# A depthwise convolution in six of eight blocks: from twelve TensorE passes to one projection, scaled copies on ScalarE and sums on GpSimd

## The chip, the cores and the metric

The kernel runs on one core of a Trainium2 chip. A core has TensorE (matrix multiply, PE in the profile, its weight loads PEld), VectorE (DVE), ScalarE (ACT), GpSimd (POOL) and SyncE (SP), which here issues every DMA. The metric is the device time of one execution in microseconds; several runs are taken, and the median counts. The profile is of one such execution.

## What is computed

Two layers over x of 4 sequences x 1024 positions x 128 channels in float32, each of the form x + s * silu(f), with s and f taken from the layer-normalised x. In the first layer s is a retention (a causal attention with decay) and f a gated network of five ternary matrices. In the second, f routes the better half of the positions through a network with a Gelu, and s is a state-space block. The part that matters here is the start of that block:

```python
x_and_gate = x @ W_in + b_in
x_ssm, gate = jnp.split(x_and_gate, 2, axis=-1)
xc = jnp.transpose(x_ssm, (0, 2, 1))
xc = lax.conv_general_dilated(xc, conv_w[:, None, :], window_strides=(1,),
        padding=[(K_ - 1, 0)], feature_group_count=D, ...) + conv_b[None, :, None]
x_conv = silu(jnp.transpose(xc, (0, 2, 1)))
BC = x_conv @ W_x + b_x
B_mat, C_mat = jnp.split(BC, 2, axis=-1)
...
h = A_discrete[None] * h + xc_t[:, :, None] * B_t[:, None, :]
y = jnp.einsum('bn,bdn->bd', C_t, h) + D_param * xc_t
...
y = y * silu(gate)
y = y @ W_out + b_out
```

So: a projection, a convolution of each channel with 4 taps back in time (zeros before the sequence), a Silu, the projections B and C, and a scan over time with 16 states for each of 128 channels.

## The kernel before

The 4096 positions are cut into 8 blocks of 512, two to a sequence (j is the block, g = 0 or 1 its place in the sequence). In most of the kernel channels or states lie on the 128 partitions and the 512 positions along the free axis. Each block goes through the same stages: ln0, retention, gated, hidden1, hidden2, out0 (the first layer), ln1, front, states, gates, router, moe, scans, project, finish, and for each sequence ranks.

The stages only record operations. A planner (Plan, lines 174 to 376) then puts them in order: it keeps for each engine the operations that can start, and picks by estimated time, then by priority. The priority comes from TIMES (lines 60 to 78), a length and eight starts for each stage; an operation inherits the lowest priority of what needs it. It also hands out buffers, a fixed number for each tag. The instructions of each engine are issued in that order and stay in it, so an instruction that waits holds up all behind it on its engine. Since all of them are issued in one loop at line 373, the profile gives them all that line, and they are told apart by the names of their tiles.

What the change touches:

- ln1 (line 793) leaves the normalised block transposed as two rounded parts, xh and xl, each with 3 columns of the block before ahead of its 512. A float32 product is made of three passes of a rounded format: high weights with high part, high weights with low part, low weights with high part (three_pass, line 676).
- front (line 812) makes the convolution in px, a PSUM bank: for each of 4 taps the input projection with that tap's weights folded in (wcv, 4 x 128 columns), on the block moved by the tap, three passes each, 12 passes of 128 x 512. At the start of a sequence the bias that the zeros would have brought in is taken off 3 columns on VectorE (edges). ScalarE's Silu, with the folded bias cbias, writes xc, and a DMA stores it to xd in DRAM.
- states (line 828) makes B and C from xc. In blocks 0 and 7 (BY_PE) TensorE spreads them over the partitions. In blocks 1 to 6, pb on TensorE is written as bc by ScalarE, stored to bd, read back spread into Br and Cr by two DMAs, and Br is copied into the one PSUM bank B by ScalarE. The tag Br has one buffer.
- scans (line 921) does 16 scans of 128 x 512 for each block. Its u tiles (two scans each, 6 buffers) are loaded from xd by DMA, multiplied by B on VectorE (u<-u,B), scanned on VectorE, multiplied by Cr on GpSimd (u<-u,Cr), and summed over the states on TensorE into py. ScalarE copies the last column (last) for the next block of the sequence. In block 7 (U_BY_PE), the first four u come from TensorE instead (pu), with the constant rep.
- gated and hidden1 split each Gelu or Silu result into parts: ScalarE casts the high part (h_h, g_h), GpSimd subtracts for the low part (h_l, g_l), and the pa and pb passes on TensorE read both.

Of the kernel before, what the change touches and what calls it, by code (L numbers as in the profile page):

```python
# [45 lines left out]
_CST = {}  # L46
_n = 0
for _name, _w in (
    ("ident", P), ("mask", P), ("tie", P), ("sel", P), ("rowdec", 1), ("coldec", 1),
):  # L50
    _CST[_name] = (_n, _n + _w)
    _n += _w
NCST = _n


ORDER = mybir.DependencyInfo(mybir.DependencyClass.NoSync, mybir.DependencyReason.DATA)
# [1 line left out]


TIMES = {  # L60
    "ln0": (10.465, (-34.463, 37.568, 0.307, -8.702, 29.140, 25.837, -0.706, 2.276)),
    "retention": (7.697, (19.747, 29.540, 0.054, 5.261, 0.588, -0.481, 27.669, 17.510)),
    "gated": (0.198, (17.080, -12.778, -2.899, 37.127, 52.075, 3.684, 35.848, 24.681)),
    "hidden1": (181979.521, (10.669, -0.997, 0.654, 26.140, 49.753, 13.692, 29.323, 21.440)),
    "hidden2": (104.604, (6.706, 7.824, 35.607, 17.363, 7.255, 8.335, 12.787, 23.305)),
    "out0": (0.269, (-10.144, 10.621, 13.685, 32.888, 37.354, 6.208, 14.587, 34.725)),
    "ln1": (0.086, (-3.447, -9.822, 3.389, 39.108, 24.646, 10.527, 7.924, 19.641)),
    "front": (99775.310, (31.104, -7.375, 49.241, 35.721, 3.625, 15.911, 8.435, 28.268)),
    "states": (1929558528.870, (-22.925, -12.719, -2.927, -2.692, -1.385, 5.843, 8.364, 33.960)),
    "gates": (2802.502, (-10.124, -3.354, -1.683, 3.017, 7.752, 67.130, 11.212, 9.313)),  # L70
    "router": (35.459, (32.003, 36.047, 1.039, 23.096, 29.397, 12.314, 55.205, 9.245)),
    "moe": (0.850, (-6.037, 10.367, -2.942, 3.023, 8.714, 12.982, 45.904, 32.432)),
    "ranks": (3.658, (7.924, -5.386, 32.363, 0.750, 18.387, 5.771, 15.184, 9.739)),
    "scans": (0.083, (26.879, 6.452, 3.058, 25.041, 26.277, 9.568, 13.774, 14.948)),
    "project": (0.218, (-2.585, 1.221, 6.521, 8.046, 9.527, 12.283, 10.650, 21.658)),
    "finish": (2311.973, (10.042, -1.800, 14.285, 18.479, 29.156, 18.433, 18.474, 24.699)),
    "load_x": (0.107, (32.705, -1.570, 6.609, 55.729, 2.835, 7.712, 33.265, 51.716)),
}
SWITCH = 0.725
SPARE = 2  # L80
XB = 5
BY_PE = (0, NBK - 1)
U_BY_PE = (NBK - 1,)
# [298 lines left out]
def tile_kernel(  # L382
# [34 lines left out]
    for name, n in {  # L417
        "x": XB, "stat0": 2, "ve0": 2, "rs0": 2, "tm0": 2, "stat1": 2, "ve1": 2, "rs1": 2, "tm1": 2, "col": 2, "wm": 2, "most": 2, "eq": 2,
        "nxt": 2, "xn0": 2, "xnT": 1, "qT": 1, "vd": 1, "sT": 1, "st": 1, "y": 1,
        "sc": 1, "xh0": 2, "xl0": 2, "sO": 2, "xh1": 2, "xl1": 2, "Br": 1, "Cr": 2, "bc": 1,  # L420
        "gate": 2, "xc": 2, "cmp": 2, "a": 3, "xn1": 3, "ff": 3, "so": 3,
        "hh": 8, "hl": 8, "h2": 5, "u": 6, "last": 2,
    }.items():
        early = name in ("a", "h2")
        plan.tag(sb, name, n, early or name in ("hh", "hl", "u"), 1 if early else None)

    def tile_(tag, name, shape=(P, HB), dtype=F32):
        if tag == "const":
            tag = name
            plan.tag(sb, tag, 1)  # L430
        return plan.tile(tag, shape, dtype, name)
# [42 lines left out]
    def vcopy(o, i):  # L474
        n = o.length() if psum(i, o) else o.length() / 2
        do("vector", "tensor_copy", o, i, cost=(n + 66) / 960)
# [20 lines left out]
    def load(name, src, shape, tag="const"):  # L497
        t = tile_(tag, name, shape)
        dma(t, src)
        return t  # L500
# [8 lines left out]
    place(-3.0)  # L509
    load_x(0)  # L510
    vec = load("vec", vecs, (P, NVEC))
    cs = load("cs", cst, (P, NCST))
    wqk_s = load("wqk_s", wqkT, (P, 2 * D), "sT")

    by_state = lambda a: a.rearrange("(e n) k -> n e k", n=NS)
    A_log = load("A_log", by_state(vecs[:, slice(*_VEC["A_log"])]), (P, NSC))
    w12_s = load("w12_s", w12T, (P, 2 * F), "sc")
    wv_t = load("wv_t", wv, (P, D))
    sel = load("sel", by_state(cst[:, slice(*_CST["sel"])]), (P, P))
    h_s = [  # L520
        [load(f"{nm}_s{k}", src[k * P : (k + 1) * P, :], (P, F), "h2") for k in range(KC)]
# [26 lines left out]
    def c(name):  # L548
        a, b = _CST[name]
        return cs[:, a:b]  # L550
# [51 lines left out]
    wB, wC = (tile_("const", name, (P, P)) for name in ("wB", "wC"))  # L602
    for w, i in ((wB, 0), (wC, NS)):
        vcopy(w.split(NS), wx_t[:, i : i + NS].stretch(E))

    rep_t = tile_("const", "rep", (P, 4 * P))
    rep = [rep_t[:, i * P : (i + 1) * P] for i in range(4)]
    for i in range(4):
        vcopy(rep[i].split(NS), c("ident")[:, 4 * i * E : (4 * i + 1) * E].repeat(NS))
    vcopy(A, logA)  # L610
    vcopy(tie, c("tie"))
    wg = split(win_s[:, D : 2 * D], "wg", (P, D))

    wcv_s = tile_("ff", "wcv_s", (P, 4, D))
    a, b = _ROW["conv_w"]
# [60 lines left out]
    def three_pass(w, xhl, cols=slice(None)):  # L676

        (wh, wl), (xh, xl) = w, xhl
        return [(wh[:, cols], xh), (wh[:, cols], xl), (wl[:, cols], xh)]
# [132 lines left out]
    def front(j):  # L812

        b, g = divmod(j, NH)
        px = mm_tile(f"px_{j}")
        terms = []
        for k in range(4):
            hi, lo = (t[:, k : k + HB] for t in R[j]["parts"])
            terms += three_pass(wcv, (hi, lo), slice(k * D, (k + 1) * D))
        passes(px, terms)  # L820
        if not g:
            vtt(px[:, 0:3], px[:, 0:3], edges, ALU.subtract)
        xc, xd = tile_("xc", f"xc_{j}"), tile_("xd", f"xd_{j}")
        act(AF.Silu, xc, px, bias=cbias)
        dma(xd, xc)
        R[j].update(xc=xc, xd=xd)

    def states(j):
        xc = R[j]["xc"]
        if j in BY_PE:  # L830
            Bp, Cr = tile_("B", f"B_{j}"), tile_("Cr", f"Cr_{j}")
            mm(Bp, wB, xc, True, True)
            if j in U_BY_PE:
                R[j]["Br"] = Br = tile_("Br", f"Br_{j}")
                act(AF.Identity, Br, Bp, bias=bB)
            act(AF.Identity, Bp, Bp, bias=bB)
            pC = mm_tile(f"pC_{j}")
            mm(pC, wC, xc, True, True)
            act(AF.Identity, Cr, pC, bias=bC)
        else:  # L840
            pb = mm_tile(f"pb_{j}", (2 * NS, HB))
            mm(pb, wx_t, xc, True, True)
            bc, bd = tile_("bc", f"bc_{j}", (2 * NS, HB)), tile_("bd", f"bd_{j}", (2 * NS, HB))
            act(AF.Identity, bc, pb, bias=v("b_x", 0, 2 * NS))
            dma(bd, bc)
            Br, Cr = tile_("Br", f"Br_{j}"), tile_("Cr", f"Cr_{j}")
            dma(Br, bd[0:NS, :].each(E), 0.63, 2.24e5)
            dma(Cr, bd[NS : 2 * NS, :].each(E), 0.63, 2.24e5)
            Bp = tile_("B", f"B_{j}")
            copy(Bp, Br)  # L850
        R[j].update(B=Bp, Cr=Cr)
# [69 lines left out]
    def scans(j):  # L921

        b, g = divmod(j, NH)
        xc, xd, Bp, Cr = (R[j][k] for k in ("xc", "xd", "B", "Cr"))
        py = tile_("py", f"py_{j}")
        last = prev.get("last")
        if not g:
            prev["last"] = tile_("last", f"last_{j}", (P, NSC))
        for m in range(4):
            us = []  # L930
            for q in range(0, 4, 2):
                ks = [4 * q + m, 4 * (q + 1) + m]
                u = tile_("u", f"u_{j}_{ks[0]}", (P, 2, HB))
                if m == 0 and j in U_BY_PE:
                    for i, k in enumerate(ks):
                        pu = mm_tile(f"pu_{j}_{k}")
                        mm(pu, rep[q + i], xc, True, True)
                        vtt(u[:, i, :], pu, R[j]["Br"], ALU.mult)
                else:
                    for i, k in enumerate(ks):  # L940
                        dma(u[:, i, :], xd[k * E : (k + 1) * E, :].whole(NS), 0.63, 2.24e5)
                    vtt(u, u, Bp.repeat(2), ALU.mult)
                for i, k in enumerate(ks):
                    do("vector", "tensor_tensor_scan", u[:, i, :], A[:, k : k + 1].bcast(HB),
                       u[:, i, :], last[:, 4 * m + q + i : 4 * m + q + i + 1] if g else 0.0, ALU.mult, ALU.add,
                       cost=(2 * HB + 104) / 960)
                if not g:
                    copy(prev["last"][:, 4 * m + q : 4 * m + q + 2], u[:, :, HB - 1])

                (vtt if j == NBK - 1 and m == 3 and q else ptt)(u, u, Cr.repeat(2), ALU.mult)  # L950
                us += [u[:, 0, :], u[:, 1, :]]
            with fused("tensor", 1.0):
                for q in range(4):
                    mm(py[32 * q : 32 * (q + 1), :], sel[:, 32 * m : 32 * (m + 1)], us[q],
                       m == 0, m == 3)
        R[j]["py"] = py
# [130 lines left out]
```

## Time and profile before

| what | value |
|---|---|
| median of 3 runs | 418.74 us (418.65 to 420.13) |
| the profiled execution | 417.93 us |
| its span, first to last instruction | 416.2 us |
| instructions | 6589 |
| mean granted TensorE clock | 0.978 |
| ACT_TABLE_LOAD on ScalarE | 39 of 1283 ns |
| xc<-px on ScalarE | 8 of 688 ns |
| px<-px,edges on VectorE | 4 of 162 ns |
| u<-u,Cr on GpSimd / on VectorE | 63 of 2389 ns / 1 of 1226 ns |
| rep<-cs on VectorE | 4 of 216 ns |
| xh and xl, 3 columns, on GpSimd | 16 of 188 to 193 ns |
| rank<-ones_bf,cmp on TensorE | 112 of 166 ns, 7 in 0.33 us |
| wgh and wgl on VectorE | 209 and 283 ns |
| u<-xd, DMA | 124 of 256 KB, 4.6 us to landing |
| Br<-bd, DMA | 6 of 256 KB, 4.3 us to landing |

How to read the lines that follow. The busy line gives each engine's busy time, its share of the span and its instructions. The rows of digits cut the span into 40 slices of 10.4 us; a digit is the busy share of a slice in tenths. A row of a group of instructions has the engine, the operation, the tiles (written <- read), the shapes, the count, then busy us and mean ns of one, then the idle time of the engine just before them and what ended it. A row of waits has who waited for whom, us in total, how many times, and the longest. TensorE's matmuls overlap, so that the record of one is longer than the time from one to the next.

### The profile page before, as it was taken

The numbers are of one execution on the slowest core, as the hardware profiler recorded it, in microseconds if no ns is written. First come the engines' busy times: TensorE is split into PE (matmuls) and PEld (weight loads), VectorE is DVE, ScalarE is ACT, GpSimd is POOL, SyncE is SP. The second block draws the span as 40 slices with busy tenths as digits, with TensorE's granted clock in tenths as the row PEclk, the third lists the DMA queues.
The fourth block names the chain that finished last, engine by engine and source line by source line (L and its number), as shares of the span: only waits on it lengthen the run. The fifth ranks groups of instructions, "written<-read, shape, count | busy, mean of one in ns | idle before, by whom it ended". The sixth has DMA issues, their size and how long they took to land.

```text
span 416.2 us, 6589 instructions
## 1 busy us (share of the span) xinstructions
PE 389.7 (94%) x2294; PEld 291.1 (70%) x2294; DVE 354.4 (85%) x621; ACT 276.3 (66%) x487; POOL 288.1 (69%) x200
## 2 busy tenths in 40 slices
PE   1999999999999999999999999999999999989843
PEld 1878878866777778777687688677877687747501
DVE  5594605996999968989999969999999999999992
ACT  3687895876557857875867598668577656772600
POOL 3066542198486897869996488967788898773890
PEclk9999999999999999999999999999999999998966
DMA  6900009206418053573602490456073553517300
GB/s 214 330 30 1 2 25 248 57 10 156 120 51 255 27 158 102 133 199 105 202 3 54 132 252 2 116 165 160 1 228 101 158 127 104 125 56 198 103 25 25
DMA packets 37897, 47.44 MB, mean 114 GB/s; under 512 B 7844, under 2 KB 17700, under 8 KB 37864
## 3 DMA queue, kind: packets, MB, share of 16 engines
q1 hardware_dynamic: 37864, 47.02, 40.8%
q8 instruction: 18, 0.29, 0.3%
q14 instruction: 15, 0.12, 0.1%
HBM read 42.40 MB, written 4.60 MB: 113 GB/s over the span
## 4 chain that ended last, share of the span: by engine, by line
PE 82%; DVE 5%; ACT 5%; POOL 4%; issue 2%; DMA 1%; POOLq 1%; SPq 1%; DVEq 0%; ACTq 0%
PE pb L373 15%; PE pa L373 12%; PE p L373 7%; PE py L373 7%; PE pg L373 6%; PE px L373 5%; PE pmo L373 5%; PE pm L373 4%; DVE u L373 4%; PE po L373 3%; POOL u L373 3%; PE pyo L373 2%; PE pv L373 2%; PE psc L373 2%; PE tr L373 2%
## 5 line engine op out<-in xcount | busy, mean ns | idle before, releaser
L373 POOL TENSOR_TENSOR u<-u,Cr 128x1024 f32<-128x1024 f32 x63 | 149.7, 2389 | 31.1 <-ACT last L373 13.0
L373 DVE TENSOR_TENSOR u<-u,B 128x1024 f32<-128x1024 f32 x62 | 73.5, 1206 | 17.1 <-DMA u<-xd 8.7
L373 DVE TENSOR_TENSOR_SCAN u<-bankA,last,u 128x512 f32<-128x512 f32 x64 | 78.5, 1266 | 0.2
L373 DVE TENSOR_TENSOR_SCAN u<-bankA,u 128x512 f32<-128x512 f32 x64 | 74.8, 1207 | 0.4
L373 POOL TENSOR_TENSOR h_l<-a,h_h 128x512 fp32r<-128x512 f32 x32 | 40.9, 1293 | 26.6 <-ACT h_h L373 26.6
L373 ACT ACT_TABLE_LOAD x39 | 50.0, 1283 | 13.6 <-PE pg L373 5.8
L373 POOL TENSOR_TENSOR g_l<-ga,g_h 128x512 fp32r<-128x512 f32 x32 | 40.6, 1293 | 20.5 <-ACT g_h L373 20.5
L373 PE MATMUL pa<-h_h,h_t 128*128 128x512 f32 x128 | 49.6, 405 | 0.0
L373 PE MATMUL pa<-h_l,h_t 128*128 128x512 f32 x128 | 48.6, 397 | 0.0
L373 PE MATMUL pb<-g_h,h_t 128*128 128x512 f32 x128 | 47.3, 396 | 0.0
L373 PE MATMUL pb<-g_l,h_t 128*128 128x512 f32 x128 | 47.1, 395 | 0.1
L373 PE MATMUL py<-u,sel 128*32 128x512 f32 x256 | 40.0, 633 | 7.2 <-POOL u L373 7.2
L373 ACT ACTIVATE h<-pb,vec 128x512 f32<-128x512 f32 x32 | 20.6, 688 | 18.1 <-PE pb L373 16.4
L373 PEld LDWEIGHTS pmo<-W_t,hm 128*128 128x128 f32 x256 | 31.1, 192 | 1.9 <-ACT ff L373 0.8
L373 PE MATMUL pmo<-W_t,hm 128*128 128x128 f32 x256 | 31.5, 275 | 0.0
L373 PEld LDWEIGHTS pg<-w_t,h 128*128 128x128 f32 x256 | 29.9, 192 | 1.0 <-ACT h L373 0.3
L373 PE MATMUL pg<-w_t,h 128*128 128x128 f32 x256 | 30.1, 275 | 0.1
L373 ACT ACTIVATE xn<-x,tm,rs 128x128 f32<-128x128 f32 x64 | 26.9, 486 | 4.6 <-DVE tm L373 4.6
L373 PEld LDWEIGHTS pa<-h_h,h_t 128*128 128x128 f32 x128 | 23.9, 188 | 7.5 <-issue 1.1
L373 PEld LDWEIGHTS pb<-g_h,h_t 128*128 128x128 f32 x128 | 23.9, 188 | 7.0 <-ACT g_h L373 1.3
L373 PEld LDWEIGHTS pa<-h_l,h_t 128*128 128x128 f32 x128 | 24.1, 188 | 6.4 <-POOL u L373 0.8
L373 PEld LDWEIGHTS pb<-g_l,h_t 128*128 128x128 f32 x128 | 23.9, 188 | 6.6 <-POOL g_l L373 1.4
(170 smaller groups left out, 838.3 us busy)
## 6 DMA issues: line engine op xcount, KB each, us to landing
u<-xd SPq DMA_DIRECT2D x124, 256.0 KB, 4.6
x<-in_x_dram SPq DMA_DIRECT2D x8, 256.0 KB, 2.9
xd<-xc SPq DMA_DIRECT2D x8, 256.0 KB, 2.0
out_dram<-x SPq DMA_DIRECT2D x8, 256.0 KB, 3.6
Br<-bd SPq DMA_DIRECT2D x6, 256.0 KB, 4.3
Cr<-bd SPq DMA_DIRECT2D x6, 256.0 KB, 5.6
h_s<-in_h1T_dram SPq DMA_DIRECT2D x4, 256.0 KB, 5.5
h_s<-in_h2T_dram SPq DMA_DIRECT2D x4, 256.0 KB, 4.2
```

The source lines that it names most:

```text
L373: i = getattr(getattr(self.nc, eng), method)(*map(real, args), **{k: real(a) for k, a in kw.items()})
```

## The change

In blocks 1 to 6, front no longer runs 12 passes. TensorE runs the three passes of the unfolded projection (wz) into px; ScalarE writes it with its bias to zc, a tile with 3 columns for the positions before; ScalarE scales zc by the last tap and adds the bias of the convolution into xc; then for each of the other three taps ScalarE writes a scaled, shifted copy into a tile of the tag Br, and GpSimd adds it to xc; at the end ScalarE takes the Silu of xc in place. The 3 columns are zeros at the start of a sequence, a copy (zh) of the last 3 of the block before, or, in block 1, three small passes (pe). Blocks 0 and 7 keep the 12 passes.

rep is no longer a constant: ScalarE writes it in block 7 into the buffer of xnT. The constant tie has a load of its own, and cs is loaded without tie and sel. All numbers of TIMES are new, so the order of all instructions is new too.

```diff
 for _name, _w in (
-    ("ident", P), ("mask", P), ("tie", P), ("sel", P), ("rowdec", 1), ("coldec", 1),
+    ("ident", P), ("mask", P), ("rowdec", 1), ("coldec", 1), ("tie", P), ("sel", P),
 ):
...
-NCST = _n
+NCST = _CST["tie"][0]
...
-    "front": (99775.310, (31.104, -7.375, 49.241, 35.721, 3.625, 15.911, 8.435, 28.268)),
+    "front": (28171.441, (9.978, 11.169, 15.771, -11.784, 20.157, 12.633, 10.937, 13.470)),
...
+TAPS_BY_PE = (0, NBK - 1)
...
-        "gate": 2, "xc": 2, "cmp": 2, "a": 3, "xn1": 3, "ff": 3, "so": 3,
+        "gate": 2, "xc": 2, "zc": 1, "zh": 2, "cmp": 2, "a": 3, "xn1": 3, "ff": 3, "so": 3,
...
-    cs = load("cs", cst, (P, NCST))
+    cs = load("cs", cst[:, 0:NCST], (P, NCST))
...
+    tie_s = load("tie_s", cst[:, slice(*_CST["tie"])], (P, P), "bc")
...
-    rep_t = tile_("const", "rep", (P, 4 * P))
-    rep = [rep_t[:, i * P : (i + 1) * P] for i in range(4)]
-    for i in range(4):
-        vcopy(rep[i].split(NS), c("ident")[:, 4 * i * E : (4 * i + 1) * E].repeat(NS))
     vcopy(A, logA)
-    vcopy(tie, c("tie"))
+    vcopy(tie, tie_s)
     wg = split(win_s[:, D : 2 * D], "wg", (P, D))
+    wz = split(win_s[:, 0:D], "wz", (P, D))
...
         px = mm_tile(f"px_{j}")
-        terms = []
-        for k in range(4):
-            hi, lo = (t[:, k : k + HB] for t in R[j]["parts"])
-            terms += three_pass(wcv, (hi, lo), slice(k * D, (k + 1) * D))
-        passes(px, terms)
-        if not g:
-            vtt(px[:, 0:3], px[:, 0:3], edges, ALU.subtract)
         xc, xd = tile_("xc", f"xc_{j}"), tile_("xd", f"xd_{j}")
-        act(AF.Silu, xc, px, bias=cbias)
+        if j in TAPS_BY_PE:
+            terms = []
+            for k in range(4):
+                hi, lo = (t[:, k : k + HB] for t in R[j]["parts"])
+                terms += three_pass(wcv, (hi, lo), slice(k * D, (k + 1) * D))
+            passes(px, terms)
+            if not g:
+                vtt(px[:, 0:3], px[:, 0:3], edges, ALU.subtract)
+            act(AF.Silu, xc, px, bias=cbias)
+        else:
+            zc = tile_("zc", f"zc_{j}", (P, 3 + HB))
+            if not g:
+                do("gpsimd", "tensor_copy", zc[:, 0:3], zero, cost=0.13)
+            elif j - 1 in TAPS_BY_PE:
+                pe = mm_tile(f"pe_{j}", (P, 4))
+                passes(pe, three_pass(wz, [t[:, 0:4] for t in R[j]["parts"]]))
+                act(AF.Identity, zc[:, 0:3], pe[:, 0:3], bias=v("b_in", 0))
+            else:
+                do("gpsimd", "tensor_copy", zc[:, 0:3], prev["zh"], cost=0.13)
+            passes(px, three_pass(wz, R[j]["x1"]))
+            act(AF.Identity, zc[:, 3 : 3 + HB], px, bias=v("b_in", 0))
+            if not g:
+                prev["zh"] = tile_("zh", f"zh_{j}", (P, 3))
+                do("gpsimd", "tensor_copy", prev["zh"], zc[:, HB : HB + 3], cost=0.13)
+            act(AF.Identity, xc, zc[:, 3 : 3 + HB], scale=v("conv_w", 3), bias=v("conv_b"))
+            for k in range(3):
+                tap = tile_("Br", f"tap_{j}_{k}")
+                act(AF.Copy, tap, zc[:, k : k + HB], scale=v("conv_w", k))
+                ptt(xc, xc, tap, ALU.add)
+            act(AF.Silu, xc, xc)
         dma(xd, xc)
...
+                rep = tile_("xnT", "rep", (P, 4, P))
+                R[j]["rep"] = rep = [rep[:, i, :] for i in range(4)]
+                for i in range(4):
+                    copy(rep[i].split(NS), ident[:, 4 * i * E : (4 * i + 1) * E].repeat(NS))
...
-                        mm(pu, rep[q + i], xc, True, True)
+                        mm(pu, R[j]["rep"][q + i], xc, True, True)
```

## The prediction

> **What bounds the kernel now.** I read the page first, then the busy time by stretch, then the chain of waits, then the groups of instructions with each shape apart, and last who waits for whom.
>
> ```profile
> PE 389.7 (94%) x2294; PEld 291.1 (70%) x2294; DVE 354.4 (85%) x621; ACT 276.3 (66%) x487; POOL 288.1 (69%) x200
> PE   1999999999999999999999999999999999989843
> DVE  5594605996999968989999969999999999999992
> PE 82%; DVE 5%; ACT 5%; POOL 4%; issue 2%; DMA 1%; POOLq 1%; SPq 1%; DVEq 0%; ACTq 0%
> ```
>
> TensorE (PE) is full from about 10 us to 395 us, and 82% of the chain that ended last is PE work. But VectorE (DVE) is nearly full too, from about 104 us on. The busy time by stretch puts numbers to it (busy us and, in brackets, instructions of PE, weight load, DVE, ACT, POOL, then granted clock, DMA share, GB/s):
>
> ```profile
> 10.40:66.10 55.70, 54.98 (x285) 45.28 (x285) 28.36 (x92) 43.64 (x73) 27.14 (x24) 1.00 0.27 85
> 66.10:104.00 37.90, 36.89 (x224) 28.39 (x223) 32.19 (x49) 28.23 (x51) 21.77 (x14) 1.00 0.43 110
> 104.00:395.00 291.00, 287.55 (x1760) 214.55 (x1758) 274.49 (x434) 199.73 (x354) 226.10 (x143) 0.99 0.45 123
> 66.10:408.60 342.50, 331.55 (x1998) 243.69 (x1996) 318.15 (x492) 228.59 (x406) 257.59 (x162) 0.98 0.43 117
> ```
>
> In the 291 us from 104 to 395, DVE has 16.5 us idle, POOL 64.9, ACT 91.3. By the timeline DVE's first scan multiply starts at 66.1, and at 408.6 only the last product with the gate is left for it; between them it idles 342.5 - 318.2 = 24.4 us. So there are two bounds: PE, with DVE close behind. Whatever PE gives up, DVE can follow only as far as those 24.4 us shrink, or its first scan comes earlier.
>
> **PE: what is removed.** Two pieces of the chain (start, length, matmuls) give the pace:
>
> ```profile
> 134.63 2.79 PE px L373 x12
> 317.85 2.57 PE px L373 x11
> ```
>
> 2.79/12 and 2.57/11 are 0.233 us for one 128x512 pass (the records say 0.40 us each, because they overlap; the pace counts). Blocks 1 to 6 go from 12 passes to 3: 6 x 9 x 0.233 = 12.6 us less. Block 1 gains three passes over 4 columns for its left edge (pe). No such shape was run: below, 7 one-column rank passes took 0.33 us (0.05 each); above, a 512-column pass, 0.233. So 0.15 to 0.7 us; I take 0.4, nearer the narrow row. Net PE: **-12.2 us**, all of it in work that is on the chain.
>
> The Trainium skill ("Perfetto Trace Analysis", section "Identifying the Most-Contended Engine") speaks against counting this as gain: matmul busy share is a poor measure, weight-load share a better one. The page here has 70% for that, and if the other 30% were free room, removing passes would be worth nothing and the time would stay at 418.7. But inside the dense px stretch a 0.188 us load comes every 0.233 us, 81%, so 74% in the middle stretch is not far from full.
>
> **ACT and POOL: what is added.** The rows that price it:
>
> ```profile
> L373 ACT ACTIVATE gate<-pt,vec 128x512 f32<-128x512 f32 x8 | 5.5, 693 | 2.3 <-PE pt L373 2.3
> L373 ACT ACTIVATE xn<-x,tm,rs 128x128 f32<-128x128 f32 x64 | 26.9, 486 | 4.6 <-DVE tm L373 4.6
> L373 ACT ACTIVATE ff<-ff,wm 128x128 f32<-128x128 f32 x32 | 11.3, 398 | 0.1
> L373 ACT ACTIVATE ff<-ff 128x512 f32<-128x512 f32 x8 | 5.0, 630 | 1.9 <-POOL ff L373 1.8
> L373 ACT CAST h_h<-a 128x512 fp32r<-128x512 f32 x32 | 19.7, 616 | 6.1 <-DVE a L373 6.1
> L373 ACT COPY last<-u 128x2 f32<-128x2 f32 x32 | 6.0, 191 | 9.6 <-DVE u L373 9.4
> L373 POOL TENSOR_TENSOR ff<-ff,xn 128x512 f32<-128x512 f32 x8 | 10.3, 1284 | 2.1 <-ACT ff L373 2.0
> ```
>
> From 2 columns (191 ns) to 512 (616 ns), ACT costs 0.833 ns a column. Per middle block: zc out of PSUM with a bias, 0.693 (the gate row, same shape). xc = scaled zc plus bias: the xn row plus 384 columns, 0.486 + 0.320 = 0.806. Three taps with a scale: 0.398 + 0.320 = 0.718 each. Silu from SBUF 0.630, in place of one of 0.688. Together 3.6 us more a block, 21.6 us in six; with block 1's edge (about 0.2) and four rep copies (below) **ACT +23 us**. POOL: 3 x 1.284 x 6 = 23.1, and eight 3-column copies (zero or zh) at the 0.19 of the xh and xl casts, 1.5: **POOL +24.6 us**.
>
> These are no cost as they stand: ACT's 91 us and POOL's 65 us of idle time in the middle stretch hold them. But POOL goes from 226 to 251 us there, which in a stretch of some 283 us is 89%, and ACT from 200 to 222, 78%. If that cover were gone, POOL's 24.6 would be more than PE's 12.2.
>
> The skill's "GPSIMD Engine Reference" ("4.1 Engine selection") would put two-input elementwise work on VectorE, since GpSimd is about twice as slow. The trace agrees on the ratio: u times Cr over 1024 columns took 2389 ns on POOL and 1226 on DVE. By the rule the 18 sums would cost 18 x 0.69 = 12.4 us of DVE, which would eat its idle time and leave no gain; on POOL they cost 23.1 us of an engine with room.
>
> **The front gets longer, and waits are added.** From first px matmul to end of xc, block 2 took 134.24 to 138.35, 4.1 us. After: three passes 0.9 (with the drain), zc 0.69, xc 0.81, then three times tap 0.72 and sum 1.28 (all taps share the one Br buffer, and each sum updates xc, so nothing of the three overlaps), Silu 0.63: 9.05, with eight hand-offs of about 0.05 (DVE's px to ACT's xc, 0.03) 9.4. So **+5.3 us** if no queue holds it up. Behind a tap that waits for POOL stand, in ACT's order, the Gelus and h_h/g_h splits that PE's pa and pb wait for and the last copies that POOL's u waits for; behind a sum that waits for ACT stand u times Cr (py on PE waits) and h_l, g_l. On SP the xd store waits for xc, and the u loads stand behind it. Who waits in the end is DVE, at the switch between blocks, for B. It already does:
>
> ```profile
> DVE u L373 <- ACT B L373: 8.3, 2, 4.1
> DVE u L373 <- DMA u<-xd: 8.7, 2, 8.3
> POOL u L373 <- ACT last L373: 13.0, 9, 2.7
> PEld py L373 <- POOL u L373: 14.7, 11, 4.6
> ```
>
> By the timeline, from the end of xc to the copy into B, blocks 1 to 6 took 19.2, 17.9, 14.0, 11.9, 11.6 and 10.6 us. In block 6 B's copy waited for Br's load, so 10.6 is the bare chain of matmul, store, load and copy. The margins are 8.6, 7.3, 3.4, 1.3, 1.0 and 0 us. Left in the old order, +5.3 would cost 1.9 + 4.0 + 4.3 + 5.3 = 15.5 us in blocks 3 to 6. But all priorities are new (TIMES). Ahead of the front, from the start of x += sO to the first xn, blocks 2 to 7 took 6.8, 9.4, 11.8, 7.1, 9.6 and 6.3 us for the same work: 0.5 to 5.5 us of queueing that another order can take out. I take the added latency as mostly covered, at a price of half of PE's gain; both ends, 0 and 15.5 us, stay in the range. The order itself no row prices: the lowest end is a first scan a few us sooner (DVE waited 8.3 for u's first load).
>
> **Small edits, together nothing.** DVE loses the edge subtractions of blocks 2, 4, 6 (3 x 0.165), and in the setup four rep copies (4 x 0.216) against two for wz (0.21 + 0.28, the wg rows): -0.9 us. rep moves to ACT in block 7, 4 x 0.30 = 1.2 us; its buffer is free when psc of block 7 has read xnT (310 us) and pu needs it at 365, so ACT's idle time there hides it; without it, up to 1.2. On SP one more load (tie, 64 KB, one issue of 0.45 us ahead of sel and the h weights) against 128 KB less in cs; the DVE casts behind waited only 0.1 to 0.3 us for h_s; up to 0.5.
>
> **The sum.** The profiled execution took 417.93 us, span 416.2 and 1.7 around it; the median shown, 418.74, is 0.8 above. PE -12.2, of which DVE and the longer front let through about half: DVE's idle time would go from 24.4 to about 18, and its largest pieces (the first u load's successors, the two B switches) do not go away by themselves. -6.5: span 409.7, median **412**. Its own range is 408.5 to 416.5.
>
> **Rivals.**
> Full gain: the new order keeps DVE fed, 418.7 - 12.2 = 406.5, with an earlier first scan 403. For it: ACT's and POOL's idle time. Against: DVE would have to be 96 to 97% busy from first scan to last.
> DVE is the bound: the PE time freed turns into waits for DVE, 417 to 420. For it: DVE 94% busy in the middle. Against: PE's 82% of the chain.
> The slower one: the tap and sum ping-pong makes B late at the switches of blocks 3 to 6. 418.7 - 12.2 + 15.5 = 422; if at each of those four switches it also stands behind one u product (2.4), 431.6; I call it 424, nearer the bare chain, since the switches have other DVE work to pull in. It decides from 4n - 5.7 = 12.2, so n = 4.5 us of front that no reordering covers. For it: margins of 0 to 1.3 us. Against: the queueing ahead of the front.
> That the passes are not saved is no rival: the loop is left out in six blocks.
>
> **How the numbers follow.** About 0.5%, 2.1 us, is what a measurement can tell from none. Forecast 0.40, full gain 0.15, DVE bound 0.17, slower 0.28: faster 0.55, same 0.17, slower 0.28. From 404 to 425, some 0.04 is left out below and 0.12 above.
>
> **What would show it.** Right: px has 2 x 12 + 6 x 3 = 42 passes and pe 3; ACT about 299 us, POOL about 312, DVE about 353 busy; DVE's idle time from first to last scan below 20. Wrong: DVE waiting 4 us or more for B at most switches, PE waiting longer for POOL's u, h_l or g_l (above 15 us in sum), or a first scan later than 66 us.

## The result and the profile after

The changed kernel took 420.02 us (median of 12 runs, 418.69 to 421.38), the kernel before in the same comparison 418.64 (418.14 to 420.25). The ratio is 1.0031, with an interval of 1.0016 to 1.0045: 1.4 us slower, less than the half per cent that counts as a difference here. The forecast was 412; the time lies inside the stated range of 404 to 425, but the gain is missing. The profiled execution took 419.78 us, its span 418.0.

From the page of the kernel after, busy time with share and instructions, the slices, and the chain that ended last:

```profile
PE 385.6 (92%) x2243; PEld 282.0 (67%) x2243; DVE 353.0 (84%) x616; ACT 295.6 (71%) x524; POOL 311.2 (74%) x226
PE   1999999999899999999999999999999999989553
DVE  4495501999659996999999999999999999999992
PE 72%; ACT 10%; DVE 7%; POOL 4%; issue 3%; DMA 2%; SPq 1%; POOLq 1%; DVEq 0%; ACTq 0%
```

The work is as forecast on every engine: ACT 295.6 us (299 was said; two table loads more than before, 2.6 us, are in it), POOL 311.2 (312), DVE 353.0 (353). The rows of the new operations, by tile (shortest, median and longest ns, then first and last start in us):

```profile
L374 ACT ACTIVATE zc<-px,vec x6: 680/688/693, 99.5 to 307.9; 128x512 f32<-128x512 f32 x6
L374 ACT ACTIVATE xc<-zc,vec x6: 814/816/836, 100.7 to 308.9; 128x512 f32<-128x512 f32 x6
L374 ACT ACTIVATE tap<-zc,vec x18: 710/726/750, 101.4 to 315.8; 128x512 f32<-128x512 f32 x18
L374 POOL TENSOR_TENSOR xc<-xc,tap x18: 1270/1290/1317, 103.7 to 316.6; 128x512 f32<-128x512 f32 x18
```

Forecast were 0.693, 0.806, 0.718 and 1.284 us. So the prices were right. What is missing is on TensorE (PE): 54 passes fewer, 12.2 us less work, and no time won. The recorded busy time fell by only 4.1 us (389.7 to 385.6), because a matmul's record (0.40 us for a 512-column pass) is longer than its pace, and covers short idle times behind it. I therefore count every matmul at the start-to-start pace of its shape (0.230 us for 128x512, 0.11 for 128x128, taken from back-to-back runs in the traces) and call the rest gaps. The end of the count is block 7's first px pass, where the work before it is nearly the same; from there to the end is the tail.

| kernel | to block 7's px, us | PE work at pace | gaps | tail |
|---|---|---|---|---|
| before | 359.8 | 336.1 | 14.3 | 56.4 |
| after | 359.5 | 327.7 | 21.7 | 58.5 |

(The remaining 9.4 and 10.1 us are the start: the first transposes begin at 9.40 and 10.10.) The work up to that point is 8.4 us less, not 12.2: 3.9 us of other matmuls were moved ahead of block 7's front by the new order. The gaps grew by 7.4 us. The tail grew by 2.1. Some of the longest waits of the kernel after, over the whole span, are these (who waited for whom; us in total, times, longest):

```profile
PEld py L374 <- POOL u L374: 18.6, 10, 4.7
PE py L374 <- POOL u L374: 8.8, 6, 3.8
PEld pb L374 <- POOL g_l L374: 5.7, 8, 1.2
PEld pa L374 <- POOL h_l L374: 2.6, 5, 0.8
DVE u L374 <- DMA u<-xd: 13.5, 2, 13.2
DVE cmp L374 <- PE rank L374: 9.1, 4, 4.6
```

The first row was 14.7 us before, the third 1.4. But the first two rows belong to the tail and not to the gaps: from block 7's front to the end the first row is, before and after,

```profile
PEld py L373 <- POOL u L373: 13.3, 7, 4.6
```

```profile
PEld py L374 <- POOL u L374: 17.8, 7, 4.7
```

and all 8.8 us of the second lie there too. Up to block 7 it is the low parts that come late: g_l with 5.7 us (1.4 before) and h_l with 2.6 (0.4 before). Beside them stands a row of the stretch from 66 to 358 us, for the weight loads of the rank (1.3 us before, up to block 7):

```profile
PEld L374 <- DVE cmp L374: 4.1, 8, 0.8
```

These are waits of the weight loads, and not all of them stop the passes: PE itself idled 1.5 us for g_l. The rest of the gaps are many short ones. VectorE (DVE) waits 13.2 us ahead of its first scan (the row with 13.2 names u's load; u had landed, and what it waited for is ScalarE's copy of B at 70.86), so the first scan product starts at 71.6 us, not 66.1. And two rank results came 3.7 and 4.6 us late for cmp. None of this is the wait for B at the switches that the slower rival named: those 8.3 us are gone.

DVE's side, by busy time in a stretch (PE, weight load, DVE, ACT, POOL, clock, DMA share, GB/s), from the first scan product to the last product with the gate, before and then after:

```profile
66.13:407.87 341.74, 331.52 (x1998) 243.66 (x1996) 317.42 (x492) 228.59 (x406) 257.59 (x162) 0.98 0.43 118
```

```profile
71.56:409.73 338.17, 322.82 (x1921) 231.42 (x1920) 317.55 (x489) 244.86 (x439) 282.39 (x190) 0.96 0.44 114
```

DVE's work is the same, its idle time fell from 24.3 to 20.6 us, and its first scan product came 5.4 us later: 5.4 - 3.7 + 0.1 = 1.8, which is the whole difference of the two spans (416.2 and 418.0). That sum says where DVE stood, not what caused it. The experiments do.

### The profile page after: what moved, and what is told of

Its sections match the earlier page's. It is cut to its first block, busy times and chain, and to the rows that moved or that the text cites. A ratio compares the mean times of both kernels' runs of the same rounds, so it can differ in the third digit from the quotient of the medians.

```text
span 418.0 us, 6549 instructions
## 1 busy us (share of the span) xinstructions
PE 385.6 (92%) x2243; PEld 282.0 (67%) x2243; DVE 353.0 (84%) x616; ACT 295.6 (71%) x524; POOL 311.2 (74%) x226
## 4 chain that ended last, share of the span: by engine, by line
PE 72%; ACT 10%; DVE 7%; POOL 4%; issue 3%; DMA 2%; SPq 1%; POOLq 1%; DVEq 0%; ACTq 0%
PE pb L374 14%; PE pa L374 11%; PE pg L374 7%; PE py L374 7%; PE p L374 6%; PE pmo L374 5%; PE pm L374 4%; DVE u L374 3%; PE po L374 3%; PE pyo L374 2%; PE px L374 2%; ACT L374 2%; PE pv L374 2%; POOL g_l L374 2%; PE tr L374 1%
## 5 line engine op out<-in xcount | busy, mean ns | idle before, releaser
L374 POOL TENSOR_TENSOR u<-u,Cr 128x1024 f32<-128x1024 f32 x63 | 149.3, 2390 | 14.9 <-DVE u L374 7.3
L374 POOL TENSOR_TENSOR g_l<-ga,g_h 128x512 fp32r<-128x512 f32 x32 | 41.1, 1311 | 16.4 <-ACT g_h L374 16.3
L374 PE MATMUL py<-u,sel 128*32 128x512 f32 x256 | 42.8, 647 | 8.8 <-POOL u L374 8.8
L374 PE MATMUL pa<-h_l,h_t 128*128 128x512 f32 x128 | 49.9, 404 | 0.0
L374 PE MATMUL pb<-g_l,h_t 128*128 128x512 f32 x128 | 48.1, 401 | 1.5 <-POOL g_l L374 1.5
L374 DVE TENSOR_SCALAR_CACHE_REDUCE cmp<-sc,col 128x1024 bf16<-128x1024 f32 (+7 forms) x32 | 25.7, 802 | 9.3 <-PE rank L374 9.1
```

Of the source, the lines that this page charges most:

```text
L374: i = getattr(getattr(self.nc, eng), method)(*map(real, args), **{k: real(a) for k, a in kw.items()})
```

## The experiments

Two theories. **Waits (W):** PE's passes hid round trips to the other engines; take the passes out and the next instruction that needs ScalarE, DVE or POOL waits instead, whichever engine is then named. **The price of the new parts (N):** the passes are worth their 12 us, and the taps, the sums, the late first scan or the new order ate them. A third, **DVE is the bound (D):** then cutting DVE's work must bring close to its full size. (The expectations, written before each run, explain letters of their own: P there says that TensorE alone sets the time, O that the order does, G that GpSimd's sums do.)

In the kernels that leave operations out, these are marked when recorded and not issued, so the order of all others stays what it was:

```diff
         for o in self.order():
+            if o.skip:
+                continue
             for r in o.allocs:
```

### Passes out, DVE's work cut, both, in the order before

The kernel before, with 9 of the 12 passes of blocks 1 to 6 not issued (54 in all):

```diff
+        n = len(plan.ops)
         passes(px, terms)
+        for o in plan.ops[n + 2 : n + 11] if 0 < j < NBK - 1 else ():
+            o.skip = True
```

> The kernel before, with every instruction in its old order, but 9 of the 12 px passes of blocks 1 to 6 left out (the output lacks those taps). Nothing is added on ScalarE or GpSimd. If TensorE alone set the time (theory P), the 12.6 us taken out come off nearly whole: -9 to -12.6 us. If VectorE sets it (theory D), only those parts of its 24.3 us of idle time between first and last scan go that were spent waiting for TensorE: -1 to -5 us.

Measured: 415.81 us against 418.45, ratio 0.9932 (0.9908 to 0.9955). So the 12.6 us of passes, with nothing in their place and no tap, no sum and no new order, are worth **2.6 us**. This alone decides most of the case for that order: the full 12 us of theory N are not there.

The kernel before, with the product u times B on 412 of each 512 columns. DVE's busy time falls by 11.3 us, from 354.4 to 343.1:

```diff
-                    vtt(u, u, Bp.repeat(2), ALU.mult)
+                    do("vector", "tensor_tensor", u[:, :, 0:412], u[:, :, 0:412],
+                       Bp[:, 0:412].repeat(2), ALU.mult, cost=(2 * HB + 62) / 960)
```

> The kernel before in its old order, but each of the 62 products u times B on VectorE covers 824 of 1024 columns (the rest of u stays unmultiplied): 62 x 200 columns at about 1.04 ns are 12.9 us less on VectorE, nothing else is changed. Theory D: -8 to -13 us. Theory P: 0 to -3 us.

Measured: 417.01 against 418.45, ratio 0.9958 (0.994 to 0.9976), **1.4 us**. And both edits together:

> The kernel before in its old order with both cuts: 54 px passes left out and u times B narrower. If the two engines bound the time together, the two gains add up to more than either alone, -14 to -22 us; theory D alone: about what the VectorE cut gives by itself plus 1 to 5 us; theory P alone: about what the passes give by themselves plus 0 to 3 us.

Measured: 412.88, ratio 0.9865 (0.9836 to 0.9894), **5.6 us**, where the two bring 4.0 alone; the intervals are too wide to tell these apart. By the expectations the first run fits their D and not P, the second P and not D: neither PE nor DVE is a bound whose work can be taken out at its price, and 12.6 and 11.3 us of work taken out together bring 5.6. The same cut of DVE in the kernel after:

> The changed kernel in its own order, with the same narrower products u times B, 12.9 us less on VectorE. Theory D (the changed kernel has TensorE time to spare, and VectorE cannot follow): -9 to -13 us, more than the same cut gives in the kernel before. Rival G (GpSimd's queue with the 18 sums sets the pace now): 0 to -4 us.

Measured: 418.03, 2.0 us below the 420.02 of the kernel after (another comparison, the same kernel before within 0.2 us; against that, ratio 0.9987, 0.9968 to 1.0006). DVE has no more weight there than before.

**Where the passes' time went** can be followed, since the first of these kernels has the order of the kernel before. I set each TensorE instruction against its twin: the lead is how much earlier it starts.

| block | lead won at px, us | given back | first TensorE instructions to wait |
|---|---|---|---|
| 1 | 2.12 | 1.36 | pb, for ACT's xc |
| 2 | 2.12 | 1.56 | pb, for ACT's xc |
| 3 | 1.87 | 1.21 | pq, for DVE's xl |
| 4 | 1.99 | 1.96 | rank, for DVE's cmp and eq |
| 5 | 2.02 | 1.47 | pa, for POOL's h_l; rank, for DVE's cmp and eq |
| 6 | 2.10 | 1.59 | py (its weight load), for POOL's u; pb, for ACT's xc |
| sum | 12.22 | 9.15 | |

Just ahead of block 1's px the second execution stood 0.26 us behind the first; 12.22 - 9.15 - 0.26 = 2.81 is the lead left behind block 6. (Only steps above 0.25 us are counted.) Each time it is taken back within a few us. Block 1 shows how. By the timeline, kernel before (start, length, instruction, and in brackets idle time before it and what ended it):

```profile
91.05 0.19 ACT L373 COPY last<-u 128x2 f32<-128x2 f32 x1 [1.24 <-DVE u L373]
91.82 0.69 ACT L373 ACTIVATE xc<-px,cbias 128x512 f32<-128x512 f32 x1 [0.58 <-PE px L373]
...
92.63 1.05 PE L373 MATMUL pb<-xc,wx_t 128*32 128x512 f32 x2
```

And with the passes out:

```profile
91.29 0.19 ACT L375 COPY last<-u 128x2 f32<-128x2 f32 x1 [1.24 <-DVE u L375]
91.39 0.68 ACT L375 ACTIVATE xc<-px,cbias 128x512 f32<-128x512 f32 x1
...
92.12 1.05 PE L375 MATMUL pb<-xc,wx_t 128*32 128x512 f32 x2 [1.29 <-ACT xc L375]
```

Before, the Silu waited for PE, and pb for nothing. Now the last px pass starts 1.86 us sooner (89.53, not 91.39), but the Silu stands behind the copy of last in ScalarE's queue, and that copy waits for DVE's scan, which is no earlier than it was. PE idles 1.29 us. In block 3 it is DVE's own queue: xl stands behind two products u times B.

```profile
174.19 2.34 DVE L375 TENSOR_TENSOR u<-u,B 128x1024 f32<-128x1024 f32 x2
176.45 0.69 DVE L375 TENSOR_TENSOR xl<-tr,xh 128x512 fp32r<-128x512 f32 x1
...
177.20 0.50 PE L375 MATMUL pq<-xl,Mh 128*128 128x512 f32 x1 [0.72 <-DVE xl L375]
```

In the kernel before PE did not idle in front of pq or of any of the others in the table (some of their weight loads waited, 0.27 to 0.36 us). What was won and not given back at a block says how close the path through the other engines lay behind PE: 0.5 to 0.8 us at five blocks, 0.03 at block 4. With DVE's cut as well, the same instructions wait nearly as long (1.36, 1.53 and 1.21 us given back in blocks 1 to 3), so 11.3 us of DVE's work bring little there: what is late is one instruction in a queue, and less work on DVE did not bring it sooner. What holds that instruction in turn was not followed further. Of the 1.4 us of the second run, all appears after 368 us, in block 7; up to there PE's starts are within 0.35 us of those before.

### The parts of the change

The kernel after, its order kept, with the 18 taps and 18 sums not issued:

```diff
+            n = len(plan.ops)
             for k in range(3):
                 tap = tile_("Br", f"tap_{j}_{k}")
                 act(AF.Copy, tap, zc[:, k : k + HB], scale=v("conv_w", k))
                 ptt(xc, xc, tap, ALU.add)
+            for o in plan.ops[n:]:
+                o.skip = True
```

> The changed kernel in its own order, with the 18 scaled copies on ScalarE and the 18 sums on GpSimd of blocks 1 to 6 left out (xc is then the Silu of one tap alone). What is left is the three passes of TensorE, zc, xc and the Silu: all of the gain and little of the cost. If the sums gave back what the passes brought (theory G): -6 to -12 us against the changed kernel, to 408 to 414. If the new order is what costs, by its late first scan and its waits for the rank (theory O): 0 to -4 us, 416 to 420.

Measured: 417.28 against 418.52, ratio 0.9965 (0.9948 to 0.9982), **2.7 us** below the kernel after. In block 1 alone (the same, with `if j == 1`):

> The same, but copies and sums are left out in block 1 alone. They stand in GpSimd's queue between the g_l subtractions from 104 to 111 us, where TensorE waits for g_l and VectorE then for the rank: 8.5 us of VectorE's idle time from 104 to 125. If the three sums make that hole and the end follows (theory G): -4 to -8 us. If the hole closes and the end does not follow, or it stays: 0 to -2 us.

Measured: 418.55, ratio 1.0 (0.9983 to 1.0018), 1.5 us below it. So 36 us of engine time (18 times 0.73 on ScalarE, 18 times 1.29 on POOL) cost 2.7 us, about half of that in one block. There GpSimd's timeline in the kernel after reads:

```profile
103.73 1.32 POOL L374 TENSOR_TENSOR xc<-xc,tap 128x512 f32<-128x512 f32 x1
105.36 1.30 POOL L374 TENSOR_TENSOR g_l<-ga,g_h 128x512 fp32r<-128x512 f32 x1 [0.31 <-ACT g_h L374]
107.07 1.29 POOL L374 TENSOR_TENSOR xc<-xc,tap 128x512 f32<-128x512 f32 x1 [0.42 <-ACT tap L374]
108.32 1.28 POOL L374 TENSOR_TENSOR g_l<-ga,g_h 128x512 fp32r<-128x512 f32 x1
109.56 1.28 POOL L374 TENSOR_TENSOR xc<-xc,tap 128x512 f32<-128x512 f32 x1
110.80 2.53 POOL L374 TENSOR_TENSOR g_l<-ga,g_h 128x512 fp32r<-128x512 f32 x2
```

Sums and low parts g_l take turns, and pb on PE waits for g_l: 0.45 us at 109.66 and 0.82 at 112.13. Without the sums these two waits are gone. The busy time of that stretch (columns as above), first in the kernel after and then with block 1's sums out, shows PE full again:

```profile
104.00:125.00 21.00, 19.73 (x136) 12.89 (x135) 12.55 (x28) 15.34 (x27) 16.08 (x12) 1.00 0.34 95
```

```profile
104.00:125.00 21.00, 21.00 (x146) 14.12 (x145) 13.76 (x37) 14.54 (x26) 13.62 (x10) 1.00 0.44 122
```

DVE is still idle for a third of this stretch, 21.00 - 13.76 us, waiting for PE's rank: the sums do not make that hole. In the kernel before cmp waited 1.4 us for the rank in the whole span, so the new order is the likely cause; no run singled it out.

The kernel after, with ScalarE's copy of B in block 0 issued before the Gelus and table loads that stood ahead of it, so that the first scan product comes at 64.65 us instead of 71.56:

> The changed kernel, one instruction moved: on ScalarE the bias of B for block 0 goes ahead of four Gelus and three table loads, from 70.9 to about 60.5 us, so that VectorE's first product u times B can start when u has landed, at about 66 and not 71.6 us. If the end follows VectorE's first scan (theory O): -3 to -5 us. If the waits further on swallow it: 0 to -2 us.

The edit, where the instructions are issued:

```diff
-        for o in self.order():
+        ops = self.order()
+        b0 = next(o for o in ops if o.eng == "scalar" and o.calls[0][2][0].root.name == "B_0")
+        ops.remove(b0)
+        at = next(i for i, o in enumerate(ops) if o.eng == "scalar" and o.calls[0][2][0].root.name == "hm_0_0")
+        mmb = max(i for i, o in enumerate(ops) if o in b0.deps)
+        ops.insert(max(at, mmb + 1), b0)
+        for o in ops:
```

Measured: 419.86, ratio to before 1.0047 (1.0027 to 1.0068), **nothing** that can be told from noise (420.02 without it). DVE's idle time between first scan and last rose from 20.6 to 27.1 us; the 7 us that it got ahead it stood waiting later. The late first scan was one of my own signs of failure, and it cost nothing.

The kernel after, with each of its three passes of blocks 1 to 6 run four times, so that PE has its 54 passes back:

```diff
+            n = len(plan.ops)
             passes(px, three_pass(wz, R[j]["x1"]))
+            for i, o in enumerate(plan.ops[n:]):
+                (eng, method, args, kw), = o.calls
+                o.calls = [(eng, method, args, dict(kw, start=i == r == 0, stop=i == 2 and r == 3)) for r in range(4)]
```

> The changed kernel in its own order, with each of the three px passes of blocks 1 to 6 run four times: the 54 passes are back on TensorE (px comes out fourfold), all copies and sums stay. If the passes saved are worth what was forecast: +6 to +12 us. If TensorE has slack that swallows them, as leaving 54 out of the kernel before gave only 2.7 us: +1 to +4 us.

Measured: 431.18, ratio to before 1.0304 (1.0281 to 1.0327), **11.2 us** above the kernel after. Adding 12.6 us to PE costs nearly all of it; taking as much out of the kernel before brought 2.6. It could be that the nine passes cost by making the front longer still, not by filling PE. The twins say no: at each of the six blocks TensorE falls 1.8 to 2.1 us behind the kernel after within the px passes themselves, and up to block 7 it makes up for less than 0.7 us of these 12.1 in all. That is what a path looks like that others follow closely: everything is behind it when it gets longer, and something else is there at once when it gets shorter. The two runs are of different kernels in different orders, so the pair shows both sides of this and not one kernel's two slopes. Nor is 431 what the long front with twelve passes would take in an order planned for them; no such kernel was run.

### The order

All numbers of TIMES are new in the change, so each comparison above of before with after has a new order in it. Three kernels got numbers of their own, found in the same way for each: the kernel after, the kernel before as control, and the kernel before with the 54 passes not recorded at all. For the kernel after the edit is the table alone, of which one line:

```diff
 TIMES = {
...
-    "front": (28171.441, (9.978, 11.169, 15.771, -11.784, 20.157, 12.633, 10.937, 13.470)),
+    "front": (2.93797039717e+57, (1649.18017987, 623.525067101, 548.796722802, -39.6165312467, 384.311939124, 323.197800714, 89.3871867335, 399.974245596)),
...
```

> The changed kernel with the same instructions and other numbers in TIMES, found by a longer search, so another order throughout. If the order is what kept the freed TensorE time from showing (theory O): -2 to -5 us against the changed kernel, 415 to 418. If the resources are used up whatever the order (theory R: TensorE's waits for VectorE and GpSimd): 419 to 421.

Measured: 416.28 against 418.24, ratio 0.9958 (0.9945 to 0.9972).

> The control: the kernel before with other numbers in TIMES from the same search for the same time. Theory O: its order was already well searched, so within 1 us of the kernel before. If a fresh order helps any kernel equally, as much less as the changed kernel gains.

Measured: 420.39, ratio 1.0041 (1.0026 to 1.0056).

Beside its table, the third has:

```diff
-        passes(px, terms)
+        passes(px, terms[:2] + terms[-1:] if 0 < j < NBK - 1 else terms)
```

> The kernel before with 9 of 12 px passes left out in blocks 1 to 6 (the output lacks those taps), nothing added, and an order searched for that work. In the old order the same cut gave 2.7 us. Theory O: a fitting order brings more, -4 to -8 us, 411 to 414.5. Theory R: no more than in the old order, -2 to -3 us.

Measured: 415.42, ratio 0.9941 (0.9923 to 0.9959).

The same computation differs by 3.7 us (after) or 2.1 us (before) with nothing but another order: as much as any step of the change. The order of the kernel after was no good one for it; with the new numbers it **beats both kernels**, 2.0 us below the one before. The control missed its expectation: it was to stay within 1 us and came out 2.1 us slower. So the search gives an order that is worse for the kernel before than the one it had, and like should be set against like. Against the kernel before in its old order the kernel without the passes wins 2.8 us, and the change 2.0. Against the control, in an order of the same search, they win 5.0 and 4.1 (420.39 less 415.42 and 416.28). So part of the small worth of the passes may be due to the order. But 5.0 us is still less than half of the 12.6 taken out, and with two or three orders for each kernel, 2 to 4 us apart, these differences are no closer than that. Last, that kernel with DVE's cut too, with an order searched for it:

> The kernel before with both cuts, 54 px passes left out and u times B on VectorE over 824 of 1024 columns, and an order searched for that work (the output lacks those taps and products). The passes alone gave 2.7 us in the old order and 2.8 in a new one. If TensorE and VectorE bound the time together (theory T), so that the passes bring little only because VectorE cannot follow, both cuts with a fitting order give -9 to -13 us, 405 to 409.5. If the waits between the engines bound it whatever their work is (theory W), no more than in the old order: -4 to -7 us, 411 to 414.5.

Measured: 412.27 against 418.35, ratio 0.9861 (0.9845 to 0.9878), 6.1 us, hardly more than the 5.6 of the old order (8.1 below the control, which is of another comparison). Here TensorE's 81% of the chain that ended last looks again like a bound:

```profile
PE 81%; ACT 7%; POOL 4%; DVE 4%; issue 2%; DMA 1%; SPq 1%; DVEq 0%; POOLq 0%; ACTq 0%
```

Which waits hold this kernel I did not settle.

**The tail** is the one place where the cut of DVE's work showed in the kernel before. From block 7's first px pass to the end, before and after (columns as above):

```profile
359.80:416.20 56.40, 40.62 (x219) 22.36 (x217) 47.94 (x66) 23.61 (x42) 32.19 (x17) 0.84 0.29 75
```

```profile
359.50:418.00 58.50, 40.76 (x194) 19.57 (x192) 50.44 (x68) 20.55 (x37) 35.12 (x19) 0.75 0.29 72
```

DVE has 2.5 us more of its work left at that point after the change, and the tail is 2.1 us longer. The reordered kernel after has 42.6 us of DVE's work left when its block 7 begins (at 362.9), and a tail of 52.5 us. But POOL too has 2.9 us more left (35.12 against 32.19), and py waits 4.5 us longer for its u, so the tail is as much POOL's as DVE's. The granted clock is lower as well, 0.75 against 0.84; it is 0.70 in the shortest of the three tails, so it does not decide alone. This is a reading of the traces; no run changed the tail alone.

## Why the prediction was wrong

**The step that failed** is the term for TensorE: "Net PE: -12.2 us, all of it in work that is on the chain", with "DVE and the longer front let through about half". The work did leave TensorE. But taken out of the kernel before with nothing in their place, the passes are worth 2.6 us in its order, less than the 6.5 that the whole change was to bring, since TensorE gave back 9.2 us of what it won in new waits for ScalarE, DVE and POOL. In an order of their own they are worth 2.8 us against the kernel before and 5.0 against the control. The sum then reads, in measured medians set against the kernel before of each comparison: 54 passes out -2.6; from there to the kernel after without taps and sums (417.28 against 418.52, so -1.2), that is zc, the small edits and the new order together, +1.4; taps and sums, +2.7; in all about +1.4. So of the 7.9 us between the forecast -6.5 and the result, half is the passes; the other half is the added work, taken as "mostly covered", and the order, of which the prediction says that no row prices it. The passes' share of the chain (82%) was read as the share of time that is theirs to give. The chain names one path; it does not say how far behind the next one is, and here that was 0.8 us or less at each block.

**The rule that was discounted was nearer.** The Trainium skill, "Perfetto Trace Analysis", section "Identifying the Most-Contended Engine", says that for TensorE matmul busy time is a poor measure of how close a kernel is to its limit, and weight-load busy share a good one. The trace has 94% for the first and 70% for the second (67% after), and if the 30% were room, the prediction said, the time would stay at 418.7. It was set aside because of the dense px stretch (81%). The time measured is within 1.4 us of it, but by luck: it is what is left of three terms. And the traces do not bear the reason out. At pace PE had work for 336.1 of the 350.4 us up to block 7, so the 30% was not free room there; and 54 passes more cost 11.2 us. PE was occupied and yet not what the end waited for alone.

**The rival "DVE is the bound", 417 to 420,** has the right time and half of the reason: freed PE time did turn into waits, in part for DVE, but cutting DVE's work by 11.3 us brings only 1.4 and 2.0. By the traces of the kernel without the passes, single late instructions in the queues, on DVE, on ScalarE behind DVE, and on POOL, hold PE.

**Taps and sums covered.** Right in kind: 36 us of work cost 2.7. The Trainium skill, "GPSIMD Engine Reference", section "4.1 Engine selection", would have two-input elementwise work on VectorE, since GpSimd is about twice as slow; the traces agree on the ratio (2390 against 1226 ns for u times Cr), but not that it decides: the 23 us of slow sums cost 2.7 with the copies that feed them. A run with them on DVE was not made.

**The front and B.** The bare front was put at 9.4 us; it took 12.0 to 16.3 (block 2), by the first px pass and the end of xc in the timeline, because taps and sums stand in line with g_l, u and Gelus. (The 134.24 that the prediction starts the old front from is the first weight load; the first px pass starts at 134.47, so the old front was 3.9 us.) That it is "mostly covered" held: DVE does not wait for B at a switch any more. The slower rival's mechanism did not occur, though its point of decision, 4.5 us of front not covered, would by length have been reached.

**The signs.** px has its 42 passes and pe 3, the three busy times are right within 4 us, DVE's idle time is 20.6 where "below 20" was said. Of the signs against, the waits of PE for POOL (above 15 us) and the first scan (71.6, later than 66) came true. The first was no sign, since it was met before the change: the three rows sum to 16.5 us in the kernel before and to 26.9 in the kernel after. What grew does contain a cost, about 1.5 us in block 1; the second is, by the run that undid it, harmless.

**Left open:** why zc and the new order cost 1.4 us, apart from the tail; what holds the late instructions on the other engines; which waits hold the kernel with both cuts at 412.3; and whether the change in its best order beats the kernel before in its best, since two orders of one kernel lie 2 to 4 us apart and few were run.

## What to carry to other kernels

Before pricing removed work by an engine's busy share or its share of the chain, ask at each place who is the next to arrive: find the first instruction behind the removed work that reads another engine's result, and see how long before its use that result was ready. Here the gain was mostly taken back there, at each of six blocks. Where engines issue in a fixed order, leave the work out and run: that one run says what the removal is worth in that order, before anything is added. Adding is not its mirror image: here it cost nearly in full (11.2 of 12.6 us, in the kernel after) where removing brought a fifth (2.6, in the kernel before). And if the order of everything changes along with an edit, run the old kernel with a new order from the same search too: here that alone was 2.1 us, more than the change, and it decides whether the change is read as 2.0 or as 4.1 us faster.

## What was not expected of the hardware

ScalarE's scaled copy with one pointer took 0.726 us and the one with scale and bias 0.816 for 512 columns, 0.09 us more where both read from SBUF (one is a Copy and the other an Identity, so the second pointer need not be all of it), and the Silu in place took 0.630. The three passes over 4 columns (pe) have records of 0.166, 0.272 and 0.252 us, far below the 0.39 of a 512-column pass.
